# Two-layer graph network on one Trainium2 core: another order for the last pieces, and the last batch left in permuted rows

## Chip, core and metric

The kernel runs on one NeuronCore of a Trainium2 chip (trn2). The metric is the device time of one execution in microseconds (us), as a median over several executions. The program is built from hand-ordered lists of steps; each engine (PE for matrix products, DVE for elementwise work, ACT for activations and copies out of PSUM, POOL for indirect transfers, SP for plain transfers) then works through its own queue in program order, and engines wait for each other through semaphores.

## What is computed

For 32 batches of a 512 x 512 float32 matrix x, with one 512 x 512 sparse matrix adj shared by all batches:

```python
# layer 0
h = relu(layernorm(x))
x = x + (adj @ h) @ W0 + b0
# layer 1: attention, with a mask that punishes every entry by its distance from 1
h = relu(layernorm(x))
q, k, v = h @ Wq, h @ Wk, h @ Wv           # 8 heads, zero biases
s = q k^T / 8 + (1 - adj) * -1e9
x = x + softmax(s) v @ Wo
```

The punishment is so steep that the softmax of a row picks the single column where adj is largest. Layer 1 is therefore a row gather: row i of the result is row idx[i] of h @ (Wv Wo), plus a constant row (cvo). The kernel decides at run time that this shortcut holds, and all that follows is in that branch ("single path", the smaller of its two sizes).

## The kernel before

**Stages of one batch.** A batch b passes through: load of x (gather on POOL), layer norm and relu into h0, aggregation adj @ h0 (`spread`, lines 637 to 656, into yT), product with W0 by a seven-piece fast matrix multiplication (`layer0`, added into x at line 584), layer norm and relu into h1 (`halves`), storing of h1 to DRAM (`put_h`), reading back only those rows that some row picks (`get_h`), transposition on DVE (`transpose_h`), product with Wv Wo in seven pieces (`layer1`, named p1, p5, u2, c11, c22, c12, c21), transposition back and writing to the DRAM tensor z (`put_z`, two parts of 4 plain transfers each), gathering each row's z back (`finish`), and storing of x to the output (`store_rows`). Three batches are in flight at different stages.

**Permuted rows.** From batch 5 on (`natural(b)` is false above FIRST = 4), the rows of a batch are held in a permuted order that makes adj block-sparse. x is gathered in that order (`plan.xi`), and the output is written by an indirect scatter on POOL to `out_rows`, the whole output seen as 16384 rows (line 512). Tables exist for reading z: `plan.place` for permuted rows, `plan.home` for natural rows. `plan.pi` and `plan.pq` hold the picked row for each natural and each permuted row. Before the change, `back(b)` is true for batches 29, 30 and 31: their x is scattered to DRAM (`turn_back`, line 468), loaded again in natural order (`come_back`, line 478), and stored by plain transfers on SP (line 510).

**The order.** For each b, `run_phase` fills 21 lists `todo[0..20]` through `put(batch, step, f, args)`. Steps 0 to 6 stand beside the pieces of `layer0(b)`, 7 to 13 beside the aggregation of b + 1 (for b = 31 beside layer 1 of batch 29), 14 to 20 beside the pieces of `layer1(b - 1)`. In each piece the generator issues the matmuls, then the step's functions, and then takes the result out of PSUM; a function at step 20 therefore stands in the queues after the matmuls of the last piece, c21. Transfers on POOL are also made to wait ("behind") for the result that was taken last. When b is 32, only the lists 0 to 20 are run, and then `layer1_rows(31)`.

**The end.** Batch 31 has its own form of layer 1: `put_h` stores the whole h1 in two transfers of 512 KB (line 679), `get_all` gathers h rows on POOL in four pieces, `transpose_all(r)` (line 711) turns them on PE with a copy on ACT, and `layer1_rows` (lines 718 to 737) does four row blocks of four matmuls each (line 723). Between the row blocks, z of batch 29 (gathered into the buffer `sel`) and of batch 30 (gathered into `yT`) is added to x on DVE (`add_z`, line 784) and stored; `fetch` issues those gathers on POOL. `put_z` of batch 30 needs all pieces of its layer 1, and its first part also the small memset on POOL of line 760.

**Waits made by the framework.** It orders any two accesses to overlapping ranges of the same tensor. The scatter of line 512 is declared to overlap the whole output; the kernel takes the waits away only between scatters (`declare_no_dep` over `stored_rows`). A plain transfer is ordered against the plain transfer eight places before it on the same kind of queue, because eight semaphores take turns.

**Near the start of the permuted part** three things are placed by step: gathers of the permuted adj rows (`Plan.tables`, POOL), gathers of extra x rows (`load_g`, POOL, into plan.gx) with a layer norm of these rows on ACT (`lead`, and `NormMore.more_stats`), and DVE's scaling for them (`lead.offset`).

The few lines which decide the end:

```python
def back(b):
    return sparse and ordered and b >= B - 3
...
put(b, 13 + c, get_all, [c])
put(b, 7 + c, turn_back, [c])
put(b - 1, 2 * c, turn_back, [c])
...
put(b - 1, 8, come_back)
put(b, 15, come_back)
...
put(b, 19, lambda b: transpose_all(0))
```

Of the kernel before, what the change touches and what calls it, by code (L numbers as in the profile page):

```python
# [408 lines left out]
def single_path(ctx: ExitStack, tc: tile.TileContext, x, adj, out, kept, room):  # L409
    nc = tc.nc  # L410
    B, N, D = x.shape
# [45 lines left out]
    def run_phase(batches, sparse, small, ps_m, ps_t):  # L457
# [3 lines left out]
            return not ordered or b <= FIRST  # L461

        def back(b):
            return sparse and ordered and b >= B - 3

        def turn_back(b, chunks):
            for c in chunks:
# [235 lines left out]

        def get_all(b, chunks=range(C)):
            for c in chunks:
                gather(hs[0][:, c, :], hs_d[b % 3], idx[:, c, 0:1] if natural(b) else plan.pi[:, c:c + 1])

        def transpose_all(r):
            pt = ps_t.tile([P, DC, P], F32, name="pt")
# [7 lines left out]
        def layer1_rows(b):  # L717
            for r in range(C):
                bank = ps_m.tile([P, D], F32, name="mm")
                for d in range(DC):  # L720
                    if d == 2 and r + 1 < C:
                        transpose_all(r + 1)
                    nc.tensor.matmul(bank, hs[1][:, d, r * P:(r + 1) * P], wvo[:, d, :], start=(d == 0),
                                     stop=(d == DC - 1))
                if sparse:
                    add_cvo(b, r)
                x_r = X[b][:, r, :].rearrange("p (q c e) -> p q c e", q=4, c=4)
                nc.vector.tensor_add(x_r, bank.rearrange("p (c q e) -> p q c e", q=4, c=4), x_r)
                if sparse and r == 0:
                    for c in range(C):  # L730
                        add_z(B - 3, c, nc.sync)
                    fetch(B - 2)
                store_rows(b, r, nc.sync)
                for i in range(2):
                    if not sparse:
                        add_z(B - 3 + r // 2, 2 * (r % 2) + i, nc.sync if r < 2 else nc.scalar)
                    elif 0 < r < C - 1:
                        add_z(B - 2, 2 * r - 2 + i, nc.sync)
# [24 lines left out]
        def put_z(b, s0, s1):  # L763
            zr = hc_t if b == B - 2 else zr_t
            nc.vector.transpose(zr[:, s0:s1, :].rearrange("p s (c e) -> p s c e", c=4),
                                zt(b)[:, :, 32 * s0:32 * s1].rearrange("p c (s j) -> p s c j", j=32))
            rows = z_d[b % 3].rearrange("(s j) (q f) -> q j s f", j=32, q=4)
            for q in range(4):
                eng = nc.scalar if q > 1 and b == B - 2 else nc.sync
                eng.dma_start(rows[q][:, s0:s1, :], zr[32 * q:32 * q + 32, s0:s1, :])  # L770

        def place_of(b, c):
# [31 lines left out]
        for b in batches:  # L804
# [6 lines left out]
            if sparse and b <= FIRST + 1:  # L811
                for j in range(3):
                    put(b + 1, 1 + j, lambda b, j: lead.stats(j), j)
                put(b + 1, 3, lambda b: lead.power())
                put(b + 1, 4, lambda b: lead.offset())
                for j in range(3):
                    put(b + 1, 4 + (j + 1) // 2, lambda b, j: lead.relu(j), j)
            if sparse:
                for j, step in enumerate((15, 17, 19) if b == FIRST else (6, 7, 8) if b == FIRST + 1 else (4, 5, 6)):
                    put(b + 2, step, load_g, [j])  # L820
# [10 lines left out]
                put(b + 2, 0, load_x)  # L831
            if b == B - 1:
                for c in range(C):
                    put(b - 2, 17 + c if sparse else 15, fetch, [c])
            elif b < B:
                for c, step in enumerate((9, 11, 13, 15) if sparse and b == FIRST + 1 else (7, 9, 11, 13) if sparse else
                                         (4, 5, 6, 7) if ordered and b == FIRST - 1 else (1, 2, 3, 4)):
                    put(b - 2, step, finish, [c])
            elif not sparse:
                put(b - 2, 1, fetch)  # L840
# [2 lines left out]
            if b > 0 and not sparse and not (ordered and b > FIRST - 3):  # L843
                put(b + 3, 15, load_x)
            if ordered and b == FIRST - 1:
                for j in range(3):
                    put(b + 2, 18 + j, load_g, [j])
            if not sparse:
                for i, step in enumerate((0, 1, 2, 3) if b != 1 else (1, 2, 3, 4)):
                    put(b + 1, step, h0_sum, i)  # L850
# [36 lines left out]
            if b < B - 1:  # L887
                put(b, 20 if not several else 17, get_h)
            elif not sparse:
                put(b, 13, get_all)  # L890
                for c in range(C):
                    put(b, 15 + c, add_cvo, c)
            elif b == B - 1:
                for c in range(C):
                    put(b, 13 + c, get_all, [c])
                    put(b, 7 + c, turn_back, [c])
                    put(b - 1, 2 * c, turn_back, [c])
                put(b - 1, 8, come_back)
                put(b, 15, come_back)
            if sparse and b == B - 2:  # L900
                for c in range(C):
                    put(b - 1, c, turn_back, [c])
# [10 lines left out]
            if b == 0:  # L913
                put(2, 1, lambda b: ahead.append(ln0(b, kind)))
                for c, step in enumerate((1, 1, 2, 2)):
                    put(2, step, lambda b, c: ahead[0].stats(c), c)
            else:
                put(b + 2, 4 if sparse else 8, lambda b: ahead.append(ln0(b, kind)))
                for c, step in enumerate((9, 10, 13, 13)):
                    put(b + 2, step, lambda b, c: ahead[0].stats(c), c)  # L920
                if kind is NormMore:
                    put(b + 2, 4, lambda b: ahead[0].more(plan.gx, plan.HG, 3))
                    for i, step in enumerate((13, 15, 17, 17, 18, 18)):
                        put(b + 2, step, lambda b, i: ahead[0].more_stats(i), i)
                    put(b + 2, 20, lambda b: ahead[0].more_power())
            put(b + 2, (17 if sparse else 15) if b > 0 else 11, lambda b: ahead[0].power())
# [10 lines left out]
                    put(0, 8, lambda b, i: sum_b(nc, w0_t, w0_s, i), i)  # L937
                    put(0, 9, lambda b, i: sum_a(nc, wvo_t, wvo, i), i)
            if b == B - 1:
                put(b, 19, lambda b: transpose_all(0))  # L940
            if b == 1:
                tables = []
                put(1, 0, lambda b: tables.append(places()))
# [70 lines left out]
FIRST = 4  # L1014


class Plan:
# [315 lines left out]
    def schedule(self):  # L1333
        def at(b, step, f, *args):
            self.steps.setdefault(b, []).append((step, lambda ps_t, behind: f(*args)))

        def pe(b, step, f, *args):
            self.steps.setdefault(b, []).append((step, lambda ps_t, behind: f(ps_t, *args)))

        def move(b, steps, f):  # L1340
            for i, step in enumerate(steps):
                self.steps.setdefault(b, []).append((step, lambda ps_t, behind, i=i: f(behind, i)))

        at(0, 0, self.load)
        at(0, 0, self.constants)
        at(0, 3, self.constants2)
        for c in range(4):
            at(0, 3 + c // 2 * 4, self.nonzero, c)
            at(0, 8 + c // 2, self.nonzero_t, c)
        at(0, 8, self.key_r)  # L1350
        for c in range(4):
            at(0, 11, self.diagonal, self.m, c)
            at(0, 12, self.diagonal, self.mt, c)
        pe(0, 11, self.rank_pe)
        at(0, 12, self.pick_r)
        k = 21
        for r in range(2):
            for go, then in ((self.sources, self.known), (self.reach, self.key_1), (self.rank_pe, self.pick_1),
                             (self.rank_pe, self.pick_2)):
                pe(*divmod(k, 21), go)  # L1360
                at(*divmod(k + 1, 21), then)
                k += 3
        at(*divmod(k - 1, 21), self.classes)
        pe(*divmod(k, 21), self.sources)
        at(*divmod(k + 1, 21), self.outside)
        k += 3
        pe(*divmod(k, 21), self.numbers)
        for i, f in enumerate((self.positions, self.positions_2, self.positions_3, self.slots)):
            at(*divmod(k + 1 + min(i, 2), 21), f)
        pe(*divmod(k + 4, 21), self.row_pe, self.pos)  # L1370
        at(*divmod(k + 5, 21), self.row_save, self.posd)
        for c in range(4):
            at(*divmod(k + 4 + c // 2, 21), self.place_onehot, c)
            at(*divmod(k + 6 + c // 2, 21), self.slot_onehot, c)
        k += 9
        pe(*divmod(k, 21), self.lists)
        at(*divmod(k + 1, 21), self.indices)
        move(2, (17, 18, 19, 20), self.rows)
        for m in range(4):
            pe(3, 4 + m, self.turn, m)  # L1380
        at(3, 6, self.save_at, 0)
        at(3, 8, self.save_at, 2)
        move(3, (11, 13, 15, 17), self.tables)
        move(4, (0, 1, 2), self.tables_g)
        for j in range(3):
            at(4, 4 + j, self.mask_g, j)
        move(5, (14, 16, 18, 20), self.look_1)
        at(6, 4, self.whole_pi)
        pe(6, 5, self.row_pe, self.pqf)
        at(6, 6, self.row_save, self.tab2)  # L1390
        move(6, (14, 16, 18, 20), self.look_2)
        at(7, 5, self.packed, self.pq, self.place)
        at(8, 5, self.packed, self.pi, self.home)
# [261 lines left out]
```

## Time and profile before

| what | us |
|---|---|
| runs, median of 3 (lowest, highest) | 1024.74 (1020.9, 1027.37) |
| the profiled execution | 1019.28 |
| its span, first to last instruction | 1017.5 |
| PE busy | 990.3 (97%) |
| DVE / POOL / ACT busy | 801.1 / 589.7 / 585.5 |
| PE idle by a wait, 300 to 960 us from the start | none listed |
| busy PE in 980 to 990 | 5.19 of 10 |
| busy PE in 1000 to 1010 | 7.66 of 10 |

Times in the views are us from the start of the span. A waits row reads "waiter <- what it waited for: us in total, times, longest". A timeline row reads "start, duration, engine, line, operation, out<-in, size, count", and in brackets the idle time of that engine just before and what ended it. A chain row has start, duration and the step. A q after an engine's name means its instruction queue, so `SPq` is a plain transfer being issued. In the names, `h<-hs,pi` is the gather of `get_all`, `sel<-z,phome` and `yT<-z,phome` those of `fetch`, `xn<-x,xi` is `turn_back`, `x<-xn` is `come_back`, and `z<-zr` and `z<-hc` are the writes of `put_z` for batches 29 and 30.

### The profile page before, as it was taken

Reading aid. Unit: us, or ns where it says so; the run is one execution under the profiler, and the core shown is the slowest. Engines: PE = TensorE matmul, PEld = TensorE weight load, DVE = VectorE, ACT = ScalarE, POOL = GpSimd, SP = SyncE. Lnnn points to the kernel's source line nnn. Section 1 sums busy time; section 2 is a strip of 40 time slices with the busy share of each in tenths; the row PEclk is TensorE's granted clock in tenths of the full one; section 3 lists DMA queues with packets and bytes.
Section 4 is the critical chain, followed back from the end, with each engine's and each line's share of the span. In section 5 each row is a group of like instructions: output and inputs, shape, how many; then the busy total and the mean of one; then the engine's idle time right before and its main releaser. Section 6 shows DMA issues by size and latency. Waiting matters only on the chain.

```text
span 1017.5 us, 17277 instructions
## 1 busy us (share of the span) xinstructions
PE 990.3 (97%) x5627; PEld 888.4 (87%) x5627; DVE 801.1 (79%) x1792; ACT 585.5 (58%) x1282; POOL 589.7 (58%) x666
## 2 busy tenths in 40 slices
PE   8999999998999999999999999999999999999986
PEld 7468888898999999999999999999999999999872
DVE  5998888667888777778887777778887777788754
ACT  3766455556765555567655555667655555676230
POOL 1033266656666666666666666666666666666552
PEclk9999999999999999999999999999999999999988
DMA  9314668888887888898888888888888888888886
GB/s 297 114 65 134 119 191 233 211 220 223 223 206 187 215 221 207 226 223 216 213 195 205 214 215 214 227 220 216 202 195 213 215 206 226 227 214 216 204 302 224
DMA packets 163035, 210.99 MB, mean 207 GB/s; under 512 B 16684, under 2 KB 104504, under 8 KB 162936
## 3 DMA queue, kind: packets, MB, share of 16 engines
q0 software_dynamic: 44544, 120.10, 48.5%
q1 hardware_dynamic: 116920, 88.29, 29.9%
q10 hardware_dynamic: 1472, 1.41, 0.4%
q8 instruction: 46, 0.75, 0.3%
q14 instruction: 53, 0.43, 0.2%
HBM read 124.60 MB, written 85.14 MB: 206 GB/s over the span
## 4 chain that ended last, share of the span: by engine, by line
PE 75%; DMA 5%; DVE 2%; ACT 2%; issue 1%; POOL 0%; SPq 0%; POOLq 0%; DVEq 0%
PE mm L528 53%; PE mm L648 13%; PE mm L651 7%; PE mm L645 2%; DMA z<-hc 1%; DMA hc<-hs 1%; DMA at<-in_x_dram,gi 1%; DMA ap<-in_adj_dram,xi 1%; DMA yT<-z,phome 1%; DMA z<-zr 1%; ACT h L379 1%; DMA hs<-h,dest 0%; ACT yT L656 0%; DMA x<-xn 0%; ACT ph L394 0%
## 5 line engine op out<-in xcount | busy, mean ns | idle before, releaser
L584 DVE TENSOR_TENSOR x<-mm,x 128x512 f32<-128x512 f32 x217 | 148.7, 686 | 133.9 <-PE mm L528 131.8
L495 POOL DMA_INDIRECT x<-z,pplace x96 | 153.4, 1598 | 81.8 <-ACT yT L656 40.9
L379 ACT ACTIVATE h<-x,off,rstd 128x512 f32<-128x512 f32 x256 | 196.1, 804 | 7.1 <-DVE off L370 3.9
L528 PE MATMUL mm<-w_t,sel 128*128 128x256 f32 x744 | 171.6, 380 | 1.0 <-DVE x L584 1.0
L365 ACT ACTIVATE rstd<-mv,eps 128x2 f32<-128x2 f32 (+1 forms) x90 | 26.3, 292 | 247.8 <-DVE mv L362 247.7
L361 DVE BATCH_NORM_STATS2 st<-x 128x6 f32<-128x512 f32 x234 | 157.6, 673 | 2.5 <-DMA x<-in_x_dram 1.5
L528 PEld LDWEIGHTS mm<-w_t,sel 128*128 128x128 f32 x744 | 140.7, 190 | 21.0 <-DVE x L584 2.0
L648 PE MATMUL mm<-ap,h 128*128 128x256 f32 x648 | 157.8, 380 | 0.0
L495 POOL DMA_INDIRECT x<-in_x_dram,xi x108 | 103.7, 960 | 73.8 <-DVE x L584 38.4
L512 POOL DMA_INDIRECT out_dram<-x,xi x96 | 120.4, 1254 | 37.3 <-DVE zs L574 20.8
L648 PEld LDWEIGHTS mm<-ap,h 128*128 128x128 f32 x648 | 114.9, 191 | 11.1
L495 POOL DMA_INDIRECT at<-in_x_dram,gi x81 | 76.7, 946 | 74.5 <-DVE st L361 26.3
L528 PE MATMUL mm<-w_s,yT 128*128 128x256 f32 x496 | 117.3, 379 | 0.8 <-ACT zs L576 0.8
L528 PE MATMUL mm<-hTs,wvo_t 128*128 128x168 f32 x720 | 115.0, 309 | 2.9 <-ACT zs L576 2.1
L528 PEld LDWEIGHTS mm<-hTs,wvo_t 128*128 128x128 f32 x720 | 106.5, 192 | 3.9 <-ACT zs L576 3.0
L576 ACT ACTIVATE zs<-mm,cvo_c 128x168 f32<-128x168 f32 x240 | 83.0, 398 | 39.0 <-PE mm L528 38.6
L528 PEld LDWEIGHTS mm<-w_s,yT 128*128 128x128 f32 x496 | 92.8, 190 | 12.3 <-ACT zs L576 1.0
L651 PEld LDWEIGHTS mm<-ag,adjT 128*128 128x128 f32 x648 | 89.3, 191 | 5.6
L651 PE MATMUL mm<-ag,adjT 128*128 128x128 f32 x648 | 89.7, 275 | 0.0
L623 DVE TENSOR_TENSOR x<-x,b_r 128x512 f32<-128x512 f32 x124 | 84.0, 678 | 0.0
L528 PE MATMUL mm<-hT,wvo 128*128 128x168 f32 x480 | 78.6, 307 | 0.0
L656 ACT COPY yT<-mm 128x512 f32<-128x512 f32 x108 | 61.6, 571 | 28.1 <-PE mm L651 27.9
(323 smaller groups left out, 1682.4 us busy)
## 6 DMA issues: line engine op xcount, KB each, us to landing
hc<-hs SPq DMA_DIRECT2D x124, 176.0 KB, 5.7
z<-zr SPq DMA_DIRECT2D x120, 96.0 KB, 3.9
hs<-h SPq DMA_DIRECT2D x52, 192.0 KB
z<-zr SPq DMA_DIRECT2D x120, 80.0 KB, 2.9
hs<-h SPq DMA_DIRECT2D x52, 160.0 KB, 3.0
out_dram<-x SPq DMA_DIRECT2D x32, 256.0 KB, 3.1
x<-in_x_dram SPq DMA_DIRECT2D x12, 256.0 KB, 4.4
x<-xn SPq DMA_DIRECT2D x12, 256.0 KB, 5.0
```

What stands on the lines that cost most here:

```text
L361: self.nc.vector.bn_stats(st, self.src[:, self.chunks[i], :])
L365: self.nc.scalar.activation(self.rstd[:, 0:len(self.chunks)], self.mv[:, :, 1], AF.Sqrt, bias=self.eps)
L379: self.nc.scalar.activation(dst, src, AF.Relu, bias=self.off[:, i:i + 1], scale=self.rstd[:, i:i + 1])
L495: return behind(nc.gpsimd.indirect_dma_start(out=dst, out_offset=None, in_=rows, in_offset=bass.IndirectOffsetOnAxis(ap=at, axis=0), **more))
L512: stored = behind(nc.gpsimd.indirect_dma_start(out=out_rows, out_offset=bass.IndirectOffsetOnAxis(ap=plan.xi[:, b, c:c + 1], axis=0), in_= ...
L528: nc.tensor.matmul(bank[:, m, 0:half], lhs[:, k, m * P:(m + 1) * P], rhs[:, k, :], start=(first and m == 0 and k == 0), stop=(k == 1), ski ...
L576: taken = nc.scalar.activation(dst[:, m, :], bank[:, m, :], AF.Identity, bias=cvo_c[:, 2 * i + m:2 * i + m + 1])
L584: return nc.vector.tensor_add(dst, bank, dst)
L623: nc.vector.tensor_add(X[b][:, c, :], X[b][:, c, :], b0_r)
L648: nc.tensor.matmul(two(bank, j), H0[b][:, j, cols], two(plan.ap[:, j, :], j), start=False, stop=False, skip_group_check=True)
L651: nc.tensor.matmul(bank[:, j * P:(j + 1) * P], extra[:, j - 1, cols], plan.ag[:, j - 1, j * P:(j + 1) * P], start=False, stop=(j == C - 1) ...
L656: tick(nc.scalar.copy(yT[:, d, :], bank))
```

## The change

1. Batch 31 is no longer turned back: `back(b)` holds for 29 and 30 only. Its four scatters to xn and four loads from xn fall away; its h rows are gathered by `plan.pq` (permuted), all four at step 13; its output goes by four POOL scatters to `out_rows`.
2. `transpose_all(0)` moves from step 19 of b = 31 to step 1 of b = 32, behind the matmuls, the copies and the first `put_z` part of layer 1 of batch 30. The four additions of cvo stand beside it, ahead of `layer1_rows`, instead of one in each row block.
3. `come_back(30)` moves from step 8 to step 16, so on SP from ahead of the h1 store and the z writes of batch 29 to behind them.
4. The writes of z of batch 30 are all issued by SP; two of four went through ACT.
5. `fetch(29)` moves from steps 17 to 20 to step 20.
6. Early: `load_g` at steps 15, 17, 18 instead of 18, 19, 20; the last two `tables` gathers at 19 and 20 instead of 15 and 17; `lead.offset` and `lead.relu` one step later; the first two `more_stats` of one batch at 15 and 16 instead of 13 and 15.

```diff
         def back(b):
-            return sparse and ordered and b >= B - 3
+            return sparse and ordered and B - 3 <= b < B - 1
...
-                gather(hs[0][:, c, :], hs_d[b % 3], idx[:, c, 0:1] if natural(b) else plan.pi[:, c:c + 1])
+                gather(hs[0][:, c, :], hs_d[b % 3], idx[:, c, 0:1] if natural(b) else plan.pq[:, c:c + 1])
...
-                if sparse:
-                    add_cvo(b, r)
...
-                eng = nc.scalar if q > 1 and b == B - 2 else nc.sync
+                eng = nc.scalar if q > 1 and b == B - 2 and not sparse else nc.sync
...
-                put(b + 1, 4, lambda b: lead.offset())
+                put(b + 1, 5, lambda b: lead.offset())
                 for j in range(3):
-                    put(b + 1, 4 + (j + 1) // 2, lambda b, j: lead.relu(j), j)
+                    put(b + 1, 5 + (j + 1) // 2, lambda b, j: lead.relu(j), j)
...
-                    put(b - 2, 17 + c if sparse else 15, fetch, [c])
+                    put(b - 2, 20 if sparse else 15, fetch, [c])
...
-                for j in range(3):
-                    put(b + 2, 18 + j, load_g, [j])
+                for j, step in enumerate((15, 17, 18)):
+                    put(b + 2, step, load_g, [j])
...
-                    put(b, 13 + c, get_all, [c])
-                    put(b, 7 + c, turn_back, [c])
+                    put(b, 13, get_all, [c])
                     put(b - 1, 2 * c, turn_back, [c])
-                put(b - 1, 8, come_back)
-                put(b, 15, come_back)
+                put(b - 1, 16, come_back)
...
-                    for i, step in enumerate((13, 15, 17, 17, 18, 18)):
+                    for i, step in enumerate((15, 16, 17, 17, 18, 18) if b == FIRST + 1 else (13, 15, 17, 17, 18, 18)):
...
-                put(b, 19, lambda b: transpose_all(0))
+                put(b, 20, lambda b: None if sparse else transpose_all(0))
+            if sparse and b == B:
+                put(b - 1, 1, lambda b: transpose_all(0))
+                for c in range(C):
+                    put(b - 1, 1, add_cvo, c)
...
-        move(3, (11, 13, 15, 17), self.tables)
+        move(3, (11, 13, 19, 20), self.tables)
```

Built, the changed program has, in the branch that runs, four transfers fewer on POOL for xn and four more for the output, four loads fewer and four output stores fewer on SP, and the same matmuls on PE in another order at the end.

## The prediction

> **What bounds the kernel now.** I read the page first: PE is busy for 990.3 of 1017.5 us, so only its gaps can be won. The waits of PE list none from 300 to 960 us. What is left is two early stretches and the end. The waits of 975 to 1018 us:
>
> ```profile
> POOL h L495 <- DMA z<-zr: 8.1, 1, 8.1
> DVE hc L765 <- ACT h0s L576: 7.2, 1, 7.2
> ...
> DVE x L784 <- DMA yT<-z,phome: 5.6, 2, 3.2
> POOL yT L495 <- DMA z<-hc: 5.2, 1, 5.2
> ...
> PE pt L711 <- DMA h<-hs,pi: 4.8, 1, 4.8
> ```
>
> They are links of one chain. The timeline of the same stretch gives the times:
>
> ```profile
> 984.89 0.84 DVE L765 STREAM_TRANSPOSE hc<-h0s 128x640 f32<-128x640 f32 x1 [0.30 <-POOL h0s L760]
> ...
> 988.79 1.11 PE L711 MATMUL pt<-ident,h 128*128 128x128 f32 x4 [4.81 <-DMA h<-hs,pi]
> ...
> 989.70 2.45 PE L528 MATMUL mm<-adjT_s,wvo 128*128 128x168 f32 x8
> ...
> 992.91 0.98 DVE L765 STREAM_TRANSPOSE hc<-h0s 128x768 f32<-128x768 f32 x1 [7.17 <-ACT h0s L576]
> ...
> 1004.26 0.69 DVE L784 TENSOR_TENSOR x<-yT,x 128x512 f32<-128x512 f32 x1 [3.18 <-DMA yT<-z,phome]
> ```
>
> The reader is to see that c21 (L528 at 989.70) stands behind a transposition that waits 4.8 us for h. The second half of z of batch 30 therefore starts at 992.91, its gather at 998.65, and the last addition at 1011.32. PE ended at 1007.66, so DVE and transfers set the end. The chain of waits says the same:
>
> ```profile
> 995.10 2.73 DMA z<-hc
> ...
> 1000.13 7.17 DMA yT<-z,phome
> ...
> 1011.32 0.69 DVE x L728
> ```
>
> Early, the timeline shows two gaps on PE:
>
> ```profile
> 189.29 0.18 DVE L404 RECIPROCAL rstd<-rstd 128x3 f32<-128x3 f32 x1 [2.99 <-ACT rstd L401]
> ...
> 190.51 1.99 PE L528 MATMUL mm<-w_t,yT 128*128 128x256 f32 x8 [1.49 <-DVE x L584]
> ...
> 235.54 2.61 PE L528 MATMUL mm<-hTs,wvo_t 128*128 128x168 f32 x8 [2.06 <-ACT zs L576]
> ```
>
> **What the Trainium skill says.** "DMA: Bandwidth & Descriptors", section "Anatomy of one DMA — SWDGE (gpsimd) path", puts a transfer from POOL at about 2.0 us plus its bytes at 436 GB/s, most of it until the receipt of the last write. For 256 KB this gives an estimate of 2.6 us; the trace's quietest scatter to xn landed in 2.7, but the median of the output scatters (L512) is 5.8 beside other traffic. The same page, "Two DMAs through the same engine are not ordered": a dependent transfer has to wait for the first one's completion semaphore. So an order between two output writes costs the whole landing, not the issue. "Issuing engines are not separate DMA queues": using ACT beside SP saves only issue time; a write of z took 0.30 to 0.52 us of SP here. "TensorE: Matmul & The Clock Gate", "What's actually happening": an idle window of about 3.4 us halves the clock. The trace agrees: PEclk is 0.50 from 988 to 992, after the 4.8 us gap.
>
> **Part 1, early.** The gathers of x rows for ACT start at 176.96, 178.22 and 179.46. At steps 15, 17 and 18 they take slots of ap gathers and move to about 172.6, 175.7 and 177.0. ACT waits 3.3 and 2.7 us for them at 181.63 and 185.89; those waits shrink, and the offset stands one addition later. The ap gathers, moved behind, land in 6.2 us (median), so near 186; PE needs them at 192.3. PE's 1.5 us gap goes. If the scaling of ag, now ahead of the offset, is late instead, nothing goes: 0 to 1.5, I take 1.5. At 235.54, ACT did a row sum (0.63 and 0.20) ahead of the copy and the activation that PE waits for. The new order puts copy and activation first: 0.8 less. PE then waits only 1.2 us, and the half clock of 235.4 to 238.4, which cost 1.6 us on two groups (2.61 and 1.63 against 1.30), should not come. But the row sums now fall between the next activations, and the group that waits for them starts near 238.1 instead of 239.41. I take 1.3, with 0 and 2.4 as ends. Sum: 2.8 us. PE is saturated from 300 to 960, so this arrives at the end whole.
>
> **Part 2, the h rows.** The h store was issued at 974.83 and 976.24, behind 1 MB of x loads at 971.15 and beside 1 MB of scatters to xn, and POOL could use it at 983.71. Both go or move. An unhindered 256 KB store lands in 2.1 us; 256 KB more at about 400 GB/s (seen at 974 to 980) makes 2.7, so 979. A gather on POOL starts 0.8 us after what it waits for (z<-hc landed at 997.83, gather at 998.65): 979.8, then every 1.25 to 984.5. The first lands 5.1 later (983.71 to 988.79 before), at 984.9. The POOL memset (0.17) is now behind all four gathers, at 984.7, so the first z transposition stays near 984.9: no gain and no loss; if h were 3 us later, it would be 3 us late.
>
> **Part 3, c21 first.** Its matmuls follow c12 at 983.82 without a gap and end at 985.0, ACT's two activations (0.69) at 985.8, DVE's second transposition at 986.8 (993.9 before). The transpositions of h follow at 985, the ACT copy (0.59) ends at 986.4, and the four row blocks take 3 x 3.88 + 3.5: PE ends near 1001.6 instead of 1007.66. With an idle time under 1 us there, the half clock does not come.
>
> **Part 4, z of batch 30.** `come_back(30)` is now ahead of it on SP. The loads go out from 981.5 to 983, landing 5.0 later (L478), to 988. The last four z writes wait for them through the shared semaphores, so they are issued up to 988.5 and land 3.5 to 4 later, near 992.3. ACT's help is replaced by about 4 x 0.4 of SP time, inside this wait. `fetch(29)` loses nothing: POOL reaches it at 985.1, and it needs z of batch 29 (last issue 981, landing 3.5). It runs from 985.5, lands by 993.5; DVE has added cvo by 989.4 and ends batch 29 at 994.3, and SP's stores land at 996.6. The yT gathers go out from 993.1 (998.65 before) to 997.8.
>
> **Part 5, the new wait.** A scatter to the output is taken to overlap every store. In the built program of the changed kernel the waits stand as follows: scatter 0 of batch 31 waits for the four stores of batch 29; stores 0 and 1 of batch 30 wait for scatters 0 and 1 to land; scatter 2 waits for these two stores; stores 2 and 3 wait for scatter 2; scatter 3 waits for them. Before, all twelve were SP stores of different rows, without such waits. Behind each waiting store, the rest of SP's queue waits, and so does POOL's queue behind each scatter; DVE is free. Prices: scatter 0.8 to start and 2.7 to land; two stores 0.05 + 0.35 + 2.1. Scatter 0 starts behind the yT gathers at 998.1, scatter 1 at 999.4, landing at 1003.0 (3.6 beside the gathers). Then 2.5 + 3.5 + 2.5 + 3.5 = 12.0: the last scatter lands at 1015.0. After it come SP's last semaphore checks and the barrier: SP's ran from 1015.5 to 1016.2 and the end was 1017.5. I take 2.3: 1017.3, 0.2 less than before.
>
> So Parts 2 to 4 win 6 us on PE and z, and Part 5 gives nearly all back. Sum: -2.8 - 0.2 = -3.0, a span of 1014.5. Against the profiled execution's 1019.28 that is 1016.3. The median of the runs, 1024.74, is 5.5 above that execution; with the same 3.0 off I forecast **1021.7**.
>
> **Rivals.** (A) The order among output writes costs nothing. Then r3 ends on DVE at 1002.6, its scatter lands at 1006.1, the end is 1008.4 (-9.1), with Part 1 -11.9: 1012.8. For it speaks the quiet end before; against it the waits in the built program. (B) The scatters are not quiet: at L512's median of 5.8 instead of 2.7, the three links cost 9.3 more, net +6.3: 1031. It decides from +1.0 each, 3.7 us. A variant lies at POOL's closing drain, 7.2 us from 1004.1, which lay under other work and would now be exposed by up to 5. Against B: only POOL and SP take turns then, with 256 to 512 KB in flight. (C) Part 1 gives nothing, because the stall moves to the ag rows or to the activations: 1024.5.
>
> **How the numbers follow.** My forecast gets 0.62 (its own range 1018 to 1026: half of Part 1, +-3 in the three landings), C 0.15, B 0.13, A 0.10. A measurement tells about 1% (10.2 us) from no change. Only A passes it downward, and by a little: faster 0.08. B's far end, with an exposed drain, passes it upward: slower 0.05. The rest is within. The range goes from 1014 to 1028: it leaves out most of A and the far half of B.
>
> **What would show it.** Right: c21 ahead of L711 near 984; no half clock at 988; h gathers from 980; yT gathers near 993; PE done near 1002; then alternating SP stores and POOL scatters, 6 us per round, with DVE idle. No waits of 1.5 and 2.1 on PE at 190 and 235. Wrong: the stores of batch 30 following their additions at once (A); scatters taking over 3.7 us each, or POOL's drain last (B); h gathers later than 983, which would move PE and z by as much.

## The result, and the profile after

The changed kernel takes 1030.91 us (median of eight runs, from 1028.17), the kernel before 1023.88 us in eight runs beside it: a ratio of 1.0081, with a 95% interval from 1.0058 to 1.0103 (the ratio on record, not the quotient of these two medians, which is 1.0069). It is 7 us slower, where 3 us less was forecast. One of the eight runs took 2117.67 us and is left out of the ratio; without it the median is 1030.17. Run a second time, on another occasion (twelfth experiment), the changed kernel took 1024.39 us against 1017.76: 1.0068 (1.0044 to 1.0093). The profiled execution took 1028.76 us with a span of 1027.0, 9.5 more than the one before.

The first thing to read is the waits from 980 us on, first those of the computing engines and POOL, then those of SP:

```profile
POOL out_dram L512 <- DMA out_dram<-x: 11.5, 2, 6.0
...
POOL yT L495 <- DMA out_dram<-x: 6.1, 1, 6.1
DVE x L782 <- DMA yT<-z,phome: 4.4, 1, 4.4
```

```profile
SPq L510 <- DMA out_dram<-x,xi: 16.0, 2, 10.6
```

PE's wait for h and DVE's for the second half of z are gone. (POOL still waits ahead of its h gathers, 10.3 us in a row left out here, but that wait ends earlier.) In their place POOL's scatters wait for plain stores of the output, and SP waits for scatters into it. The second row of POOL is to be read with care: a store landed just before the gather started, but what that gather waits for are the writes of z, whose last one landed at 997.87, 1.0 us ahead of it. The chain of waits shows the scatters and stores as links of one chain:

```profile
1003.91 1.32 POOL out_dram L512
...
1005.54 3.44 DMA out_dram<-x,xi
...
1009.54 2.31 DMA out_dram<-x
...
1012.64 2.72 DMA out_dram<-x,xi
...
1015.83 2.62 DMA out_dram<-x
...
1019.24 0.96 POOL out_dram L512
```

From the second scatter on it is scatter, store, scatter, store, scatter: no piece of computing lies between. What the change was to win on PE is there. The timeline of PE after:

```profile
985.32 1.30 PE L528 MATMUL mm<-adjT_s,wvo 128*128 128x168 f32 x8
986.46 0.60 PE L711 MATMUL pt<-ident,h 128*128 128x128 f32 x4
988.48 1.98 PE L723 MATMUL mm<-wvo,h 128*128 128x512 f32 x4 [1.42 <-ACT h L712]
...
998.48 5.32 PE L723 MATMUL mm<-wvo,h 128*128 128x512 f32 x12
```

c21 now stands ahead of the transposition, the 4.8 us wait for h is gone, and PE ends at 1003.8 instead of 1007.66. But the last 23 us of the span hold no work of PE at all.

At the very end stands POOL's closing drain. Its row in the source view (times it occurs; shortest, median and longest in ns; first and last start) is this before:

```profile
L1650 POOLq DRAIN  x3: 51/103/7215, 1004.1 to 1017.2; - x3
```

and this after:

```profile
L1650 POOLq DRAIN  x3: 51/103/4591, 1021.6 to 1026.8; - x3
```

Before, it began at 1004.1 and was over at 1011.3, under DVE's last additions. Now it begins after the last transfer has been issued and runs in the open. SP has nothing left to do at 1022.6 and waits for the barrier until the drain is over at 1026.2. The view shows this as a wait of 3.8 us, which it puts down to PE, whose work was long done:

```profile
SPq L1650 <- PEq L1650: 4.3, 2, 3.8
```

To compare executions whose early parts differ, I count from the first layer-1 group of batch 29 (before: 969.00; after: 969.80; second trace of the changed kernel: 965.65):

| from that group, us | before | predicted | after | after, second trace |
|---|---|---|---|---|
| first h gather | 14.7 | 10.8 | 11.6 | 11.4 |
| first z write of batch 30 | 16.8 | 16.8 | 18.9 | 17.2 |
| first yT gather | 29.7 | 24.1 | 29.1 | 27.8 |
| scatter 0 issued | none | 29.1 | 34.1 | 32.8 |
| last scatter issued | none | 43.3 | 49.4 | 47.5 |
| end of the span | 48.5 | 48.3 | 57.2 | 55.4 |

The forecast column is that of the prediction in the clock of before, less 969.00. Two entries are worked out: the first z write is its transposition at 984.9 and the 0.9 us that lay between the two before, and the last scatter's issue is its landing at 1015.0 less 2.7.

### The profile page after: what moved, and what is told of

It reads as the page before. It is cut to its first block, busy times and chain, and to the rows that moved or that the text cites. A ratio compares the mean times of both kernels' runs of the same rounds, so it can differ in the third digit from the quotient of the medians.

```text
span 1027.0 us, 17270 instructions
## 1 busy us (share of the span) xinstructions
PE 988.8 (96%) x5627; PEld 886.7 (86%) x5627; DVE 801.3 (78%) x1792; ACT 585.3 (57%) x1282; POOL 591.0 (58%) x666
## 4 chain that ended last, share of the span: by engine, by line
PE 85%; DVE 5%; DMA 5%; issue 2%; ACT 1%; POOL 1%; SPq 0%; ACTq 0%; POOLq 0%; DVEq 0%
PE mm L528 61%; PE mm L648 13%; PE mm L651 7%; PE mm L645 2%; PE mm L669 1%; DMA x<-in_x_dram 1%; DMA ap<-in_adj_dram,xi 1%; DMA out_dram<-x 1%; ACT h L379 1%; PE mm L271 1%; DVE st L361 1%; DMA out_dram<-x,xi 1%; DMA sel<-z,phome 1%; DMA x<-in_L_gnn_Wo_dram 0%; ACT yT L656 0%
## 5 line engine op out<-in xcount | busy, mean ns | idle before, releaser
L512 POOL DMA_INDIRECT out_dram<-x,xi x100 | 124.6, 1246 | 49.5 <-DVE zs L574 13.9
```

What stands on the lines that cost most here:

```text
L512: stored = behind(nc.gpsimd.indirect_dma_start(out=out_rows, out_offset=bass.IndirectOffsetOnAxis(ap=plan.xi[:, b, c:c + 1], axis=0), in_= ...
```

## Experiments

The theory from these views: the order among output writes and the drain behind it take back what the tail wins; the z writes are late for a reason still open; the early edits win nothing. The rivals are named with each run. All ratios are to the kernel before on the same chip.

**1. No order among the output writes.** The changed kernel with, in `store_rows`, the plain stores of batches 29 and 30 and the scatters of batch 31 declared independent:

```diff
+                if back(b):
+                    for scattered in LAST:
+                        tc.declare_no_dep(plain.ins, scattered.ins, reason="other rows")
+                    PLAIN.append(plain)
...
+            if sparse and b == B - 1:
+                for plain in PLAIN:
+                    tc.declare_no_dep(stored.ins, plain.ins, reason="other rows")
+                LAST.append(stored)
```

> The changed kernel; only the waits between the plain output stores of batches 29 and 30 and the four output scatters of batch 31 are taken away (the rows are disjoint). Theory (these waits and the drain behind the last scatter give the end back): all four scatters follow the yT gathers, 1004 to 1008.7, the last landing near 1010.5, the drain of POOL of 4.6 to 7.2 us after it: the span falls by 10 to 13 us, to 1014 to 1017. Rival (the order costs little, the end is late because z of batch 30 and its gathers are late): no more than 4 us less.

Measured: 1020.36 us, ratio 0.9987 (0.9972 to 1.0002), against 1.0081 and 1.0068 with the order: 8 to 10 us. The span was 1017.5, the stretch of the table 47.4. In POOL's timeline the scatters follow each other:

```profile
1002.51 0.99 POOL L516 DMA_INDIRECT out_dram<-x,xi  x1 [0.30 <-issue]
...
1003.81 0.98 POOL L516 DMA_INDIRECT out_dram<-x,xi  x1 [0.19 <-issue]
...
1009.10 0.96 POOL L516 DMA_INDIRECT out_dram<-x,xi  x1 [2.93 <-DVE x L734]
```

The last one waits for DVE, no longer for a store. The theory holds, though the span fell by 9.5 us, a little less than the 10 to 13 expected. But without the order the change only equals the kernel before; the 6 us of Parts 2 to 4 are not all there.

**2. c21 first, alone.** The kernel before with one edit, batch 31 still turned back:

```diff
-                put(b, 19, lambda b: transpose_all(0))
+            if sparse and b == B:
+                put(b - 1, 1, lambda b: transpose_all(0))
```

> The kernel before; only the transposition of the first h rows of batch 31 moves behind the last piece of layer 1 of batch 30. Batch 31 is still turned back and stored by plain transfers. Theory: the 4.8 us wait of PE stays, but c21 is no longer behind it; the second part of z starts 6 to 9 us earlier, and without any order among output writes this arrives at the end: 4 to 6 us less than before, a span near 1012. Rival: the z writes of batch 30 are bound to the x loads through the shared semaphores anyway: 0 to 2 us less.

Measured: 1022.07 us, ratio 1.0019 (1.0004 to 1.0034). No gain, rather a loss, and both expectations were wrong. ACT's timeline, then PE's:

```profile
992.12 3.39 ACTq L770 DMA_DIRECT2D z<-hc  x2
995.55 0.59 ACT L712 COPY h<-pt 128x512 f32<-128x512 f32 x1 [4.48 <-DMA z<-hc]
```

```profile
992.26 1.12 PE L711 MATMUL pt<-ident,h 128*128 128x128 f32 x4 [3.22 <-DMA h<-hs,pi]
996.19 3.78 PE L723 MATMUL mm<-wvo,h 128*128 128x512 f32 x4 [2.82 <-issue]
```

ACT issues two z writes, which wait for their semaphores; the copy of h that PE needs stands behind them in ACT's queue. PE waits 2.8 us more, and its clock is at 0.50 from 992 to 1000.

**3. The early edits alone.** The kernel before with item 6 of the change (`load_g`, `tables`, `lead`, `more_stats` at their new steps).

> The kernel before with only the early edits (item 6). As predicted: 2.8 us less than before. Rival 1 (the stalls only change place, as the trace of the changed kernel has it): 0 to 1 us more, with PE waits near 180, 219 and 267. Rival 2 (those three stalls are not made by the edits but come and go from one execution to the next): 1 to 3 us less in the median, and other places of the stalls in this trace.

Measured: 1021.69 us against 1020.68, ratio 1.0008 (0.9990 to 1.0027). The 2.8 us forecast, 0.9973, lie outside the interval. (On this chip the two gaps that Part 1 priced do not stand even in the old order; see the twelfth.)

**4. The change without the early edits.** Item 6 taken back.

> The changed kernel with the early edits (item 6) taken back. If the early edits are worth what was predicted, 2.8 us more than the changed kernel; if they are worth nothing, the same within 1 us; if they cost, 1 us less. The end (yT gathers, scatters and stores in turn, drain) should be as in the changed kernel: 46 to 50 us from the first layer-1 group of batch 29 at 970 to the end less what comes before, so yT gathers 29 us and the last scatter 49 us behind that group.

Measured: 1029.19 us, ratio 1.0072 (1.0046 to 1.0097): the changed kernel's own ratio. yT gathers 27.7 and last scatter 48.9 us behind the group, end 56.8.

**5. The x loads of batch 30 behind its z writes.** The changed kernel with

```diff
-                put(b - 1, 16, come_back)
...
+                put(b - 2, 1, come_back)
```

(the second line in the list of b = 32).

> The changed kernel; only the four x loads of batch 30 (come_back) move on SP from ahead of its z writes to behind them. Theory (the last z writes were late because they take turns on the semaphores with these loads, and every link behind them is late by as much): yT gathers near 994 instead of 999. What follows is the point: scatter 0 of batch 31 also waits for the stores of batch 29, which land near 1000, so it can start only near 1001 instead of 1004; with the order among the output writes unchanged the end is 3 us earlier, a median of 1026 where the kernel before has 1021. Rival (the z writes are late because DMA is full): yT gathers within 1 us of the changed kernel, no gain.

Measured: 1027.66 us, ratio 1.0092 (1.0068 to 1.0116). From first z write to first yT gather it took 10.2 us; the changed kernel has 10.2 and 10.6 in its two traces. The rival stands: it is not the semaphores shared with these loads. The second trace of the changed kernel shows it directly, since its z writes wait only 0.7 us for the loads:

```profile
SPq L768 <- DMA x<-xn: 0.7, 2, 0.5
```

**6. c21 first, and all z writes from SP.** The second experiment with item 4 of the change added:

```diff
-                eng = nc.scalar if q > 1 and b == B - 2 else nc.sync
+                eng = nc.scalar if q > 1 and b == B - 2 and not sparse else nc.sync
```

> The second experiment (the kernel before, c21 first) with one more edit: the four z writes of batch 30 that ACT issued go out from SP. Theory (in the second experiment ACT's queue stood at its two last z writes for 3.4 us, and the copy of h that PE waits for stood behind them): the copy follows the transposition within 1.5 us, no 2.8 us gap of PE at the first row block, 3 to 6 us less than in the second experiment. Rival (the late h rows set the end, whoever issues): within 1 us of it.

Measured: 1015.89 us against 1018.08, ratio 0.9984 (0.9968 to 1.0000): 3.6 us less than the second experiment. The copy on ACT and PE behind it:

```profile
987.81 0.59 ACT L712 COPY h<-pt 128x512 f32<-128x512 f32 x1 [4.71 <-PE pt L711]
```

```profile
987.11 0.67 PE L711 MATMUL pt<-ident,h 128*128 128x128 f32 x4 [4.74 <-DMA h<-hs,pi]
988.45 2.08 PE L723 MATMUL mm<-wvo,h 128*128 128x512 f32 x2 [0.68 <-ACT h L712]
```

So item 4, which I had costed at 4 x 0.4 us of SP and nothing more, takes away what item 2 costs alone; whether the two together gain anything, 1.6 us here, is at the edge of the noise. The Trainium skill ("DMA: Bandwidth & Descriptors", section "Issuing engines are not separate DMA queues") has a second issuer save issue time only; in these two runs the second issuer also cost something, since an issue that waited held all that stood behind it on ACT, for 3.4 us.

**7. Scatters ahead of the additions of batch 30.** The first experiment with `elif r > 1` in `layer1_rows`, two additions of batch 30 each behind row blocks 2 and 3, instead of 1 and 2.

> The kernel of the first experiment (no order among the output writes); the additions of z of batch 30 stand behind all four row blocks of batch 31, so that the four scatters of batch 31 stand ahead of them. Theory (POOL's closing drain has a fixed length of 4.6 us from 1.4 us behind its last issue, and so the last scatter's issue sets the end): last scatter issued near 1006.3 instead of 1009.1, the end 2 to 3.5 us earlier than in the first experiment. Rival (the drain waits for all transfers, and the last store ends): no gain, since the last yT gather still lands at 1007.5.

("Behind all four row blocks" is not what this kernel has: two additions stand behind block 2 and two behind block 3.) Measured: 1012.92 us against 1018.08, ratio 0.9955 (0.9935 to 0.9975): 3.3 us under the first experiment, though the two intervals still touch. The last scatter stands 35.5 us behind the group instead of 39.0, the end 45.8 instead of 47.4.

**8. All together.** The seventh with the edit of the fifth, and `store_rows(b, 0)` ahead of the yT gathers.

> A version meant to beat both: no order among the output writes, the x loads of batch 30 behind its z writes, scatter 0 of batch 31 ahead of the yT gathers, two additions of batch 30 behind row block 2 and two behind row block 3. Theory: yT gathers near 994, PE done near 1003.5, last scatter issued by 1005, drain to 1011, a span near 1012.5 to 1013.5 at the early stalls of the first experiment: 4 to 5 us under the kernel before. Rival: DMA is full there, the gathers land late, no better than the experiment before it.

Measured: 1013.44 us, ratio 0.9955 (0.9939 to 0.9971), no better than the seventh. yT gathers 26.9 us behind the group, not 24.

**9. Without the sel gathers.** The changed kernel without `fetch(29)` and its four additions; its output lacks z of batch 29.

> The changed kernel without the four gathers of z of batch 29 into sel (1 MB) and their additions: z of batch 29 is not added to x. The first z write of batch 30 and the first yT gather were 10.2 to 10.4 us apart in the changed kernel and in the first, fourth and fifth experiments, wherever the x loads stood. Theory (the DMA engines are full from 984 to 996, and the sel gathers, put right there, take the share that the z writes need): 6 to 7.5 us apart, so the yT gathers and all that follows 3 to 4 us earlier, the end too. Rival (eight z writes of 512-byte rows take that long by themselves): still 10 us apart, no gain at the end.

Measured: 1024.46 us against 1019.84, ratio 1.0042 (1.0025 to 1.0059), so 2.7 to 4 us less than the changed kernel by the ratios, whose intervals overlap in part. From first z write to first yT gather it took 7.6 us instead of 10.2 to 10.6. The windows view (the last two numbers are the busy share of the DMA engines and GB/s), first of the changed kernel's first trace, where the first z write stands at 988.72:

```profile
988.00:992.00 4.00, 3.52 (x11) 1.83 (x12) 3.93 (x6) 1.01 (x2) 3.07 (x4) 1.00 1.06 383
992.00:996.00 4.00, 4.00 (x14) 2.01 (x13) 1.98 (x3) 0.59 (x1) 0.80 (x1) 1.00 1.01 296
```

and of this run, where it stands at 985.89, so that its rows are to be read some 3 us earlier:

```profile
984.00:988.00 4.00, 3.18 (x15) 2.00 (x15) 3.45 (x6) 1.17 (x3) 0.98 (x2) 1.00 1.03 353
988.00:992.00 4.00, 4.00 (x14) 1.97 (x13) 1.80 (x3) 0.58 (x1) 0.00 (x0) 1.00 1.01 326
992.00:996.00 4.00, 4.00 (x15) 2.04 (x14) 0.69 (x1) 0.59 (x1) 1.89 (x2) 1.00 0.72 250
```

The DMA engines are full in both for some 8 us from the first z write; the stores of batch 29 fill what the gathers leave. What differs is who stands ahead: the last z write landed 2.7 us after its issue here, and 5.7 and 5.4 us after it in the two traces of the changed kernel. Little of this reached the end of the trace. Against the second trace of the changed kernel, the yT gathers are 3.1 us earlier, but the last scatter only 0.5 (47.0 us behind the group) and the end 0.6 (54.8), because the second scatter took 4.7 us to land.

**10. One switch instead of five.** The changed kernel, all waits kept, the scatters behind all plain stores in program order (the `store_rows` of batch 31 in a loop of their own at the end).

> The changed kernel with all its waits among output writes, but the four scatters of batch 31 stand behind all plain stores of batches 29 and 30 in program order, instead of in turn with them. Theory (each change between plain store and scatter costs a whole landing, 2.3 to 3.4 us, and the last scatter's issue plus 7.8 us is the end): stores of batch 30 follow their additions, landing by 1010.5; then four scatters 1.25 us apart, 1011 to 1015; the end at 1022.5 to 1023.5, 4 us less than the changed kernel, and still 2 to 4 us over the kernel before. Rival (the number of changes does not matter, only that POOL is last): within 1.5 us of the changed kernel.

Measured: 1021.94 us against 1019.84, ratio 1.0032 (1.0016 to 1.0048), 4 to 5 us less than the changed kernel, as expected. POOL's timeline:

```profile
1007.18 0.98 POOL L512 DMA_INDIRECT out_dram<-x,xi  x1 [8.32 <-issue]
...
1011.02 0.96 POOL L512 DMA_INDIRECT out_dram<-x,xi  x1 [0.19 <-issue]
```

From the first to the last scatter it is 3.8 us, where it was 15.3 in turn with stores. The end stands 8.2 us behind the last issue.

**11. The eighth, with all four additions of batch 30 behind row block 3.**

> The eighth experiment with all four additions of batch 30 behind row block 3, so that the last scatter does not stand behind an addition that waits for yT. Theory (last scatter's issue sets the end): last scatter 34.5 us behind the first layer-1 group of batch 29 instead of 35.6, the end 1 us earlier, 0.5 to 0.6% under the kernel before. Rival (the plain stores of batch 30, now behind it, end last): no gain or 1 us more.

Measured: 1014.27 us against 1019.84, ratio 0.9949 (0.9934 to 0.9965). The last scatter stands 35.2 us behind the group, 0.5 earlier than in the eighth, the end 44.5, 0.1 later: no gain shown.

**12. The changed kernel again, for its trace.**

> The changed kernel once more, unchanged, for its trace. In its first trace DVE paused three times for 1.9 to 2.7 us with nothing that it waited for (before 218.6, 257.3 and 987.2), and the engines 2 to 2.6 us at the branch near 179. Theory (these pauses belong to one execution and not to the edits): other places and lengths of the pauses, the first layer-1 group of batch 29 between 966 and 971.5 as in the other runs, the stretch from it to the end near 56 us instead of 57.2 if the pause at 987 is missing. Rival (they belong to the layout of the program): the same pauses at the same instructions, 969.8 and 57.2 within 0.3 us. In both cases the ratio to the kernel before is 1.006 to 1.010.

The first trace has these waits on PE early, and these pauses of DVE:

```profile
180.01 3.07 PE L528 MATMUL mm<-w_s,yT 128*128 128x256 f32 x8 [2.39 <-issue]
...
219.39 1.99 PE L528 MATMUL mm<-w_t,sel 128*128 128x256 f32 x8 [1.70 <-DVE x L584]
...
266.75 1.41 PE L528 MATMUL mm<-hTs,wvo_t 128*128 128x168 f32 x8 [1.84 <-ACT zs L576]
```

```profile
218.64 1.29 DVE L584 TENSOR_TENSOR x<-mm,x 128x512 f32<-128x512 f32 x2 [3.68 <-PE mm L528]
...
257.29 0.69 DVE L584 TENSOR_TENSOR x<-mm,x 128x512 f32<-128x512 f32 x1 [2.62 <-PE mm L645]
```

The second trace, of the same program, has other waits on PE from 170 to 300:

```profile
177.39 1.99 PE L528 MATMUL mm<-w_s,yT 128*128 128x256 f32 x8 [0.78 <-ACT zs L576]
188.26 1.99 PE L528 MATMUL mm<-w_t,yT 128*128 128x256 f32 x8 [0.24 <-DVE x L584]
230.32 1.38 PE L528 MATMUL mm<-hTs,wvo_t 128*128 128x168 f32 x8 [1.20 <-DVE hTs L341]
233.14 1.41 PE L528 MATMUL mm<-hTs,wvo_t 128*128 128x168 f32 x8 [1.45 <-ACT zs L576]
```

None of the three pauses came again, and the group of batch 29 began at 965.65 instead of 969.80. The kernel before's early part did the same in three executions: 969.00, 971.52 (second experiment) and 966.25 (sixth). So one trace of this kernel cannot tell 3 us in its early part.

There is a pattern in it. Waits of PE near 180, 220 and 267 stand in the first trace of the changed kernel and in all four traces of experiments 1 to 4, which ran on one chip, and in none of the nine other traces. The second and the fourth experiment have the early edits left out and show them all the same:

```profile
181.72 2.98 PE L528 MATMUL mm<-w_s,yT 128*128 128x256 f32 x8 [3.31 <-ACT zs L576]
221.02 1.99 PE L528 MATMUL mm<-w_t,sel 128*128 128x256 f32 x8 [1.61 <-DVE x L584]
268.45 1.41 PE L528 MATMUL mm<-hTs,wvo_t 128*128 128x168 f32 x8 [1.52 <-ACT zs L576]
```

These rows are of the second. So the early edits do not make these waits; whether that chip does, or the occasion, was not tried.

## Why the prediction was wrong

The forecast was -3.0 us; the medians say +7.0, and +6.6 in the second set. With the second trace's stretches, the 10 us between them come from four terms of the sum: 2.8 of Part 1, 3.7 of Part 4, 0.5 of Part 5's rounds and 2.9 of its closing, 9.9 in all.

**Part 1 (-2.8) was not found.** Alone the early edits measure +0.8 us (interval -1.0 to +2.8), and the change costs the same without them (fourth). But both ran on the chip where the gaps at 190 and 235 do not stand in the old order either (second), so they do not test the two gaps as such. On other chips the working holds in part: in the second trace of the changed kernel the gap at 190 is down to 0.24, but the gap at 235 becomes two, 1.20 and 1.45. The sixth experiment has the old order and the same 2.06 us wait at 234, without the half clock; the 1.6 us that I counted for it belonged to one execution. From the group near 178 us (`w_s,yT`) to the first layer-1 group of batch 29 the old order took 790.6 and 787.7 us (before, sixth) and the new one 787.5 to 791.0 in the seven traces on other chips, so no gain shows there. The failed step is to price an edit from gaps of a single execution in a stretch whose start at the tail differs by 5 us between executions.

**Part 2 was right but for the memset.** h gathers at 10.8 from the group, measured 11.4 to 11.6. The memset behind them moved with them: in the second trace DVE waits 0.73 us for it, and the first z write stands 0.4 later than before.

**Part 3 was right.** c21 ahead of L711, no half clock before PE ends, PE done 32.6 from the group, measured 32.7 in the second trace (34.0 in the first, with a pause of DVE at 987).

**Part 4 failed: "The last four z writes wait for them through the shared semaphores, so they are issued up to 988.5 and land 3.5 to 4 later, near 992.3."** In the second trace the eight writes go out from 17.2 to 21.7 us behind the group, each taking 0.3 to 0.7 us of SP (forecast: to 19.5), and the last lands 5.4 us after its issue, at 26.7, 1.0 ahead of the yT gather (forecast: 3.5 to 4, at 23.3). The cause I gave is wrong as well: SP waited 0.7 us for the x loads, and moving them away left the stretch as it was (fifth). The z writes share full DMA engines with the sel gathers (ninth: 7.6 us from write to gather without them, 10.2 to 10.6 with them). I had written that `fetch(29)` loses nothing, and so priced its own wait only, not what its 1 MB takes from others. The yT gathers came at 27.8 instead of 24.1. That these 3.7 us reach the end whole is worked out, not shown: the ninth took 3.1 us off the gathers and 0.6 off the end of its trace.

**Part 5: the mechanism was right, two sizes were not.** The waits stand as worked out, and they are the cause: without them 8 to 10 us less (first), with one switch 4 to 5 us less (tenth). The rounds took 14.7 us in the second trace and 15.3 in the first, against 14.2. In the last round of the first trace, from 1012.64 to 1019.24, the scatter landed in 2.72 and POOL started 0.79 after the store's landing, as taken; but the second store landed in 2.62 us, not in 2.1, and was issued 0.48 after the scatter's landing, not 0.40. The closing was the larger miss: "After it come SP's last semaphore checks and the barrier ... I take 2.3." After the last landing it was 5.1 to 5.2; before, with the drain hidden, 2.5. The reason was in my text, as a variant of rival B: POOL issues last, so its drain is exposed. It takes 4.3 to 4.6 us in all ten traces with scatters at the end, begins 1.3 us behind POOL's last instruction in the first trace of the changed kernel, and the end comes 7.7 to 8.2 us behind the last scatter's issue wherever the order was kept. That it sets the end is read from SP's wait for the barrier; no run hid the drain again. I took the row of before, 7.2 us hidden, as a rival only, although "POOL issues last" was certain in the new order.

**The rivals.** A is wrong: the order costs 8 to 10 us, and even without it the end stands 47.4 us behind the group (first), where A had 39.4. B's main form is wrong: the three scatters of the chain landed in 2.7 us, or 3.4 beside another, not in 5.8. B's variant, the exposed drain, is right, with 2.9 us of the up to 5 that I gave it. C has the size of Part 1 right and, with the gap at 235 that became two, a part of its reason; about the rest it is wrong.

**Where the gain went.** PE is done 32.7 to 34.0 us behind the group instead of 38.7, so the 5 to 6 us there are real, but PE does not decide the end. They were turned into waits among output writes, and into a drain that had been hidden. When the order is taken away and the scatters stand earlier (seventh), 4.6 us under the kernel before appear (0.45%, 0.25 to 0.65), with the drain still in the open. There the DMA share is 0.73 to 1.07 from 980 to 1004, in the eighth 0.89 to 1.02, which fits the eighth and eleventh giving nothing more; that this is the bound there was not tried. The end stands 8.7 to 10.3 us behind the last scatter's issue in those three, instead of about 8. The scatter itself took 4.5 to 5.3 us to land there, instead of 2.7, and the drain, of its usual length, began later too, 0.9 to 1.8 us ahead of that landing. What starts the drain stays open.

## What to carry to other kernels

Before part of a result is moved from plain stores to indirect scatters, list the waits that the framework makes between the two kinds: each change of kind cost a whole landing, and a declared independence took away 8 to 10 us here, one change of kind instead of five 4 to 5. Ask which engine issues last and what closing work it has, since a cost that lay hidden comes into the open when another engine becomes the last. And a gain of 3 us read from gaps in one execution needs a second execution, on another chip too, before it enters a sum.

## What the runs showed of the hardware

POOL's closing drain, when scatters come last, was 4.59 or 4.60 us in nine of ten traces and 4.26 in the ninth experiment; when gathers of z came last it was 7.0 to 7.8 us and lay under other work. Waits of PE near 180 us (2.2 to 4.6 us), 220 (0.9 to 1.7) and 267 (0.9 to 1.8) came in the four traces of one chip and in the first trace of the changed kernel, with the early edits and without, and in none of nine others, one of them of the same program; their cause is open. How long a transfer took to land went with what was in flight beside it: the last z write 5.4 to 5.7 us with the sel gathers and 2.7 without them, and the last scatter 2.7 us in the changed kernel, where the DMA share was 0.25 at that time, and 4.5 to 5.3 us in the seventh, eighth and eleventh, where it was 0.74 to 0.92.
